# Gelu of a transformer's MLP from Square, Tanh and two VectorE operations instead of one table function

## The chip, the cores and the metric

The kernel runs on one core of a Trainium2 chip. The time is the device time of one execution in microseconds, and of several executions the median counts. The five engines are TensorE (PE; its weight loads are listed as PEld), VectorE (DVE), ScalarE (ACT), GpSimd (POOL) and SyncE (SP), which here only issues the transfers of the DMA queue. Each engine runs its instructions in the order in which the program gives them.

## The reference

Two transformer layers over 2048 rows of 256 numbers, with 16 heads of 16, and with 1601 rows of context in the second layer. All is float32.

```python
# layer 0: adaptive norm from c (ada_w, ada_b), two halves x0, x1 of 1024 rows
x0 = x0 + g_msa[0] * mha(mod(ln(x0), ...));  x1 = x1 + g_msa[1] * mha(mod(ln(x1), ...))
ox = attend(qx, ky, vy) @ crs_proj_w + crs_proj_b    # each half attends to the other
oy = attend(qy, kx, vx) @ crs_proj_w + crs_proj_b
x = x + concat(g_mca[0] * ox, g_mca[1] * oy)
def mlp(z):                                          # 256 -> 1024 -> 256
    return gelu(z @ mlp_fc1_w + mlp_fc1_b, approximate=True) @ mlp_fc2_w + mlp_fc2_b
x = x + concat(g_mlp[0] * mlp(mod(ln(x[:1024]), ...)), g_mlp[1] * mlp(mod(ln(x[1024:]), ...)))
# layer 1
x = layernorm(x + mha(x, x, x, mask))                # masked self-attention
x = layernorm(x + mha(x, ctx, ctx))                  # attention to the context
x = layernorm(x + relu(x @ w1 + b1) @ w2 + b2)
```

`gelu(..., approximate=True)` is 0.5 x (1 + tanh(sqrt(2/pi) (x + 0.044715 x^3))).

## The kernel before

**Stages.** There are four attention stages: 0 (self-attention of the halves), 1 (cross-attention of the halves), 2 (masked) and 3 (context). The rows are cut into four blocks of 512 (`BLK`). A unit of work is one block and one of four groups of four heads, and `stream` runs all units of all stages in one sequence of steps. One step of unit u does four things: the scores of a later unit, for their maxima (`maxima`: two matmuls of L860, then on DVE one reduction, L875, or in the masked stage two pairs of L868); the transposed scores of u, less the maxima (`weights_of`: L938, L945, in the masked stage also L953) with the Exp on ACT (L958); a share of the product with the values (`values_of`: L975); and one piece of background work. Each pair of scores takes one of three PSUM buffers `s_ps`, which L860 and L938 use in turn; the sums of the unit and the background pieces share the two PSUM banks `m0` and `m1`, one each, which change roles from unit to unit. `as_rows` (L899, then the copy `nm` on ACT, L904) also uses the bank of the background work.

**Background.** When the last group of a block is through, `chain_after` hangs a chain of pieces into the background: projection, residual, normalization, the MLP, and keys, values and queries of the next stage. A chain is a generator. A `piece` yields before it takes its bank, then issues its matmuls, yields, and one step later issues what takes the result out of the bank. Steps with other turns on the bank (L899) hold a piece back, and when a unit ends and the bank changes roles, `flush` issues what is unfinished at once. So the chain's place in the order of every engine comes from the number of its yields.

**The MLP.** `mlp` runs for each block twice: with Gelu in `chain_cross` (stage 1, four blocks; the fourth block's chain runs beside the first units of the masked stage), and with Relu in `chain_last`. The first layer has eight pieces: two matmuls (L515) into the bank, then `take` on ACT (L523) with the bias of the column `cols[:, ci + f]` into one of eight tiles `hid`. While `stream` runs, `take` is only an Identity for the Gelu, and the eight Gelus stand inside the second layer, each ahead of the first matmul that reads its tile (L534, L535). The second layer has four quarters of eight tiles (16 matmul records each, L535), and `gated` adds the result to the block (L478 on DVE, L479 and L481 on POOL); then L553 stores the block.

**Start.** Before any stage, SP issues in this order: `c`, the first rows of x, ada weights and biases, more of x, the raw weights of stage 0 (`w_raw`, `w_v`, `bv`), then `cols` (L261, the biases of both first layers) and the small transfers of `qkb` (L269). Meanwhile PE multiplies ada (L284): DVE copies the transposed `c` into `cT` (L278), and each product goes through one bank to DVE (L288). Normalization, products, stores and loads of keys follow in one chain.

**Keys on their way.** The new keys and queries go out as a rounded part and a rest: `hi` on ACT (L392), `lo` on DVE (L393), each into one of three buffers of the tag `half`, from which SP stores them (`k_dr`, `q_dr`, L397). They come back for the next stage as `kT` (L712) and `q` (L771). SP issues all of them in one order with the mask loads (`raw`, L804, two buffers, cast on POOL by L805), the sums (L1013, L1022), their inverses (L1044, L1046) and, in the split first block of the masked stage, the maxima (`mh`, L911). The tag `stage` has two buffers, for the normalized block, the values on their way out, raw weights and context rows.

Of the kernel before, what the change touches and what calls it, by code (L numbers as in the profile page):

```python
# [16 lines left out]
AF = mybir.ActivationFunctionType  # L17
ALU = mybir.AluOpType
# [4 lines left out]
P = 128  # L23
# [6 lines left out]
DFF = 1024  # L30
BLK = 512
# [45 lines left out]
def two_layers(ctx: ExitStack, tc: tile.TileContext, a: dict, out: bass.AP):  # L77
    nc = tc.nc
# [18 lines left out]
    streaming = [False]  # L97
# [13 lines left out]
    def one_ps(dtype=F32, n=None):  # L111
        n = small[0] if n is None else n
        flush((n,))
        return ps.tile([P, BLK], dtype, tag=f"m{n}", bufs=1, name=f"m{n}_ps")
# [3 lines left out]
    def piece(*steps):  # L118

        yield BANK  # L120
        if streaming[0]:
            n = small[0]
            m = one_ps(n=n)
        else:
            n = None
            while len([e for e in unfinished if e[0] is None]) > 2:
                flush_one()
            m = ps.tile([P, 2, BLK], F32, tag="s", bufs=3, name="s_ps")[:, 0, :]
        left = [lambda f=f: f(m) for f in steps[1:]]
        entry = (n, left)  # L130
        unfinished.append(entry)
        steps[0](m)
        while left:

            yield 1 if len(left) > 1 else 0
            if left:
                left.pop(0)()
        if entry in unfinished:
            unfinished.remove(entry)

    def flush_one():
        entry = next(e for e in unfinished if e[0] is None)
        unfinished.remove(entry)
        while entry[1]:
            entry[1].pop(0)()
# [42 lines left out]
    def stage(shape, dtype=F32, name="t"):  # L188
        return sb.tile(shape, dtype, tag="stage", bufs=2, name=name)
# [4 lines left out]
    def hidden(shape, dtype=F32, name="hid"):  # L194
        return sb.tile(shape, dtype, tag="hidden", bufs=HB, name=name)
# [64 lines left out]
    cols = sb.tile([P, 16], F32, tag="cols", name="cols")  # L260
    nc.sync.dma_start(cols, a["cols"][:, 32:])  # L261

    qkb = sb.tile([P, 4, 2, 2], F32, tag="qkb", name="qkb")
    src = a["cols"][:, :32].rearrange("(c i r) (t w g) -> g i c r t w", c=2, i=2, t=4, w=2)
    for g in range(NG):
# [8 lines left out]
    m = one_ps()  # L274
# [6 lines left out]
    for n0, n, w, ada_b in ada:  # L281
        m = one_ps()
# [223 lines left out]
    def mlp(w, ci, func, hT, finish, between=None):  # L506
        w1, w2 = w
        hid: list = [None] * (DFF // P)


        wait = func != AF.Relu and streaming[0]

        def up(m, f):
            for k in range(2):
                nc.tensor.matmul(  # L515
                    m, lhsT=w1[k][:, f * P : (f + 1) * P], rhs=hT[:, k, :],
                    start=k == 0, stop=k == 1,
                )

        def take(m, f):  # L520
            hid[f] = hidden([P, BLK])
            bias = cols[:, ci + f : ci + f + 1]
            nc.scalar.activation(hid[f], m, AF.Identity if wait else func, bias=bias)  # L523

        for f in range(DFF // P):
            yield from piece(lambda m, f=f: up(m, f), lambda m, f=f: take(m, f))
        if between is not None:
            between()

        def down(m, n, q2):  # L530
            qt = 2 * n + q2
            for f in range(DFF // P):
                if wait and qt == 0:
                    nc.scalar.activation(hid[f], hid[f], func)  # L534
                nc.tensor.matmul(  # L535
                    m[:, q2 * D : (q2 + 1) * D], lhsT=hid[f][:, qt * P : (qt + 1) * P],
                    rhs=w2[f // 4][:, f % 4, :], start=f == 0, stop=f == DFF // P - 1,
                )

        for n in range(2):  # L540
            yield from piece(
                *(lambda m, n=n, q2=q2: down(m, n, q2) for q2 in range(2)),
                lambda m, n=n: finish(n, m.rearrange("p (t d) -> p t d", d=D)),
            )
# [41 lines left out]
    def chain_cross(b):  # L586

        last = b == ORDER[1][-1]
        t = residual(x_in(b))
        yield from project(1, b, gated(rows["a1"], t, b))  # L590
        if last:
            load_output(2)
            rows["a2"] = load_rows(7, 3)
        yield 2
        xn = stage([P, TPB, D], name="xn")
        yield from normalize(xn, t, 1e-6)
        hT = yield from transposed(xn, mod=(2, b // 2))
        yield from mlp(
            mlp0, 0, AF.Gelu_apprx_tanh, hT, gated(rows["m0"], t, b),

            (lambda: mask_part(1)) if last else None,
        )
        if last:
            rows["a3"] = load_rows(10, 3)
        kept((2, b), t)
        yield 2
        hT = yield from transposed(t)
        yield from keys_and_values(2, hT, b)
        yield from halves(2, 0, hT, b, BLK)
        if last:  # L610
            background.extend([chain_context(n), 0, False] for n in range(NB))
# [36 lines left out]
    def chain_last(b):  # L648

        t = residual(xs[3, b])  # L650
        yield from project(3, b, biased(rows["a3"], t))
        yield 3
        yield from post_norm(rows["a3"], t)
        hT = yield from transposed(t)
        yield from mlp(mlp1[0], 8, AF.Relu, hT, biased(rows["m1"], t))
        yield 3
        yield from post_norm(rows["m1"], t)
        nc.sync.dma_start(out[b * BLK : (b + 1) * BLK, :].rearrange("(t p) d -> p t d", p=P), t)
# [676 lines left out]
```

## Time and profile before

| | |
|---|---|
| median of 3 runs | 3392.64 us (3391.25 to 3396.46) |
| the profiled execution | 3403.53 us, span 3401.7 us from the first to the last instruction |
| granted TensorE clock, mean over the span | 0.968 |
| busy: PE, DVE, ACT, POOL | 92%, 62%, 50%, 12% of the span |
| transfers of the DMA queue | 187.57 MB, 22.3% of 16 engines' span |
| Gelu (L534), 32 instructions | 17.1 us on ACT, 615 ns each |
| table loads on ACT | 10, at 1283 ns; 4 before a Gelu, 5 before an Exp, 1 before the Silu |

A profile line of a group gives engine, line, operation, what it writes and reads with shapes, how often, the busy time in us and the mean in ns, then the engine's idle time just before these instructions and what ended it. A timeline line gives start, length, engine, line, operation and, in brackets, the idle time before it with what ended it. A busy PE is not PE at its peak, since ends of matmuls are modelled. PE, ACT and DVE work on different steps at once, so the idle time of ACT or DVE costs nothing by itself; idle time of PE does.

### The profile page before, as it was taken

The page shows a single profiled execution, that of the slowest core. Times are in us where ns is not written, and L with a number is a line of the kernel's source. Part 1 is how long each engine was busy: PE and PEld are TensorE (multiplying, and loading weights), DVE is VectorE, ACT ScalarE, POOL GpSimd, SP SyncE. Part 2 cuts the span into 40 slices and gives each one's busy share as a digit, 9 for nine tenths or more (in the row PEclk, how much of TensorE's full clock was granted, in tenths as well). Part 3 has the DMA queues.
Part 4 walks back from the last instruction along what each step waited for, and adds up shares of the span by engine and source line. Part 5 has one row for each costly group of instructions (what it writes and reads, how often), then busy time and mean ns, then how long its engine had stood idle before and what let it go on. Part 6 is the DMA issues. An engine that isn't in the chain of part 4 may idle for free.

```text
span 3401.7 us, 56761 instructions
## 1 busy us (share of the span) xinstructions
PE 3113.2 (92%) x22592; PEld 1362.0 (40%) x22592; DVE 2120.7 (62%) x3858; ACT 1713.7 (50%) x1868; POOL 404.6 (12%) x344
## 2 busy tenths in 40 slices
PE   4799999998999889898999999999999999999995
PEld 2334444444444433333333333343334444444433
DVE  2676766764646455366767777767656747657541
ACT  1265655655545445343555555554546646546461
POOL 0001101101010121104023012201010011110102
PEclk8799999999999999899999999999999999999997
DMA  5652162160204121343111001102241100000000
GB/s 177 140 105 65 36 117 65 48 128 24 65 18 114 32 84 37 94 100 107 51 39 51 15 20 58 32 17 55 49 87 43 26 10 26 25 18 26 10 14 16
DMA packets 162362, 191.20 MB, mean 56 GB/s; under 512 B 82584, under 2 KB 95520, under 8 KB 162096
## 3 DMA queue, kind: packets, MB, share of 16 engines
q1 hardware_dynamic: 162096, 187.57, 22.3%
q8 instruction: 178, 2.92, 0.4%
q14 instruction: 88, 0.72, 0.1%
HBM read 129.91 MB, written 48.46 MB: 52 GB/s over the span
## 4 chain that ended last, share of the span: by engine, by line
PE 51%; DVE 5%; ACT 4%; DMA 2%; SPq 2%; POOL 1%; issue 1%; ACTq 0%; POOLq 0%; DVEq 0%
PE m_ps L975 13%; PE s_ps L938 8%; PE s_ps L860 8%; PE s_ps L953 7%; PE s_ps L945 6%; ACT e L958 3%; PE m_ps L515 2%; DVE s_ps L868 2%; PE m_ps L535 2%; DVE pm L875 1%; PE m_ps L460 1%; DMA raw<-in_mask 1%; PE m_ps L385 1%; DVE t L328 1%; PE m_ps L415 1%
## 5 line engine op out<-in xcount | busy, mean ns | idle before, releaser
L958 ACT ACTIVATE e<-s_ps 128x1024 f32<-128x1024 f32 (+1 forms) x1440 | 1468.1, 1025 | 1375.0 <-PE s_ps L945 794.8
L875 DVE TENSOR_REDUCE pm<-s_ps 128x2 f32<-128x1024 f32 (+3 forms) x1024 | 1120.9, 1106 | 534.7 <-PE s_ps L860 530.2
L975 PE MATMUL m_ps<-e,V 128*32 128x256 f32 (+2 forms) x10432 | 903.6, 418 | 7.3 <-ACT hT L354 4.4
L868 DVE CUSTOM_DVE_ANT_0 s_ps<-s_ps,bias 128x512 f32<-128x512 f32 x1024 | 712.8, 701 | 295.4 <-PE s_ps L860 161.6
L860 PE MATMUL s_ps<-kT,q 64*128 64x512 f32 (+3 forms) x3072 | 676.6, 443 | 111.8 <-ACT e L958 51.1
L938 PE MATMUL s_ps<-q,kT 64*128 64x512 f32 (+1 forms) x2880 | 677.3, 466 | 51.8 <-ACT e L958 28.4
L945 PE MATMUL s_ps<-nm,sel 64*128 64x512 f32 (+1 forms) x2880 | 575.2, 395 | 0.1
L860 PEld LDWEIGHTS s_ps<-kT,q 64*128 64x128 f32 x3072 | 294.1, 186 | 528.1 <-issue 301.1
L938 PEld LDWEIGHTS s_ps<-q,kT 64*128 64x128 f32 (+1 forms) x2880 | 270.5, 184 | 496.6 <-issue 241.0
L975 PEld LDWEIGHTS m_ps<-e,V 128*32 128x32 f32 (+1 forms) x10432 | 206.9, 108 | 433.6 <-issue 415.3
L953 PE MATMUL s_ps<-biasT,ident 128*128 128x512 bf16 x1024 | 311.4, 386 | 0.0
L1053 POOL TENSOR_TENSOR oT<-oT,rd_rows 64x512 f32<-64x512 f32 x64 | 81.7, 1277 | 1904.8 <-DMA rd_rows<-rd_dr 1491.1
L945 PEld LDWEIGHTS s_ps<-nm,sel 64*128 64x128 f32 (+1 forms) x2880 | 275.2, 187 | 12.1 <-ACT nm L904 0.8
L805 POOL TENSOR_SCALAR bias<-raw 128x512 bf16<-128x512 int32 x64 | 123.1, 1924 | 266.4 <-DMA raw<-in_mask 256.4
L868 DVE DVE_READ_ACCUMULATOR2_ANT pm<- 128x1 f32 x1024 | 144.9, 141 | 0.0
L953 PEld LDWEIGHTS <-ident 128*128 128x128 bf16 x1024 | 58.4, 97 | 187.8 <-issue 187.8
L393 DVE SCALAR_TENSOR_TENSOR lo<-m_ps,qkb,hi 128x512 fp32r<-128x512 f32 (+2 forms) x56 | 41.1, 734 | 137.3 <-ACT hi L392 94.3
L535 PE MATMUL m_ps<-w_mlp,hid 128*128 128x256 f32 x448 | 111.4, 405 | 11.9 <-ACT hid L534 11.9
L385 PE MATMUL m_ps<-hT,w_qk 128*128 128x512 f32 (+2 forms) x224 | 109.8, 613 | 9.3 <-DVE lo L393 8.8
L515 PE MATMUL m_ps<-hT,w_mlp 128*128 128x512 f32 x224 | 111.0, 618 | 1.1 <-ACT hT L354 1.1
L535 PEld LDWEIGHTS m_ps<-w_mlp,hid 128*128 128x128 f32 x448 | 86.3, 200 | 36.5 <-ACT hid L534 16.3
L415 PE MATMUL m_ps<-w_v,hT 128*128 128x256 f32 (+1 forms) x212 | 58.0, 420 | 21.8 <-DVE lo L393 21.4
(106 smaller groups left out, 1220.9 us busy)
## 6 DMA issues: line engine op xcount, KB each, us to landing
q<-q_dr SPq DMA_DIRECT2D x544, 64.0 KB
kT<-k_dr SPq DMA_DIRECT2D x192, 128.0 KB
raw<-in_mask SPq DMA_DIRECT2D x64, 256.0 KB
q_dr<-hi SPq DMA_DIRECT2D x32, 256.0 KB
q_dr<-lo SPq DMA_DIRECT2D x32, 256.0 KB
oT<-sums SPq DMA_DIRECT2D x256, 32.0 KB
rd_rows<-rd_dr SPq DMA_DIRECT2D x64, 128.0 KB
v_dr<-v SPq DMA_DIRECT2D x14, 544.0 KB
```

What stands on the lines that cost most here:

```text
L385: nc.tensor.matmul(m[:, :n], lhsT=wqk[:, k, w, c, :], rhs=hT[:, k, :n], start=k == 0, stop=k == 1)
L515: nc.tensor.matmul(m, lhsT=w1[k][:, f * P : (f + 1) * P], rhs=hT[:, k, :], start=k == 0, stop=k == 1,)
L535: nc.tensor.matmul(m[:, q2 * D : (q2 + 1) * D], lhsT=hid[f][:, qt * P : (qt + 1) * P], rhs=w2[f // 4][:, f % 4, :], start=f == 0, stop=f = ...
L805: nc.gpsimd.tensor_scalar(bias_rows[b, slot, qt][:, j * BLK : (j + 1) * BLK], raw, 0.0, MASKED, ALU.is_equal, ALU.mult,)
L860: nc.tensor.matmul(s[:, h, :nn], lhsT=u["q"][64 * h : 64 * h + 64, i, qt * P : (qt + 1) * P], rhs=kT[g][slot][64 * h : 64 * h + 64, i, c : ...
L868: nc.vector.tensor_tensor_reduce(out=s[:, h, :], in0=s[:, h, :], in1=bias_rows[b, slot, qt][:, c : c + nn], scale=1.0, scalar=-3.0e38, op0 ...
L875: nc.vector.tensor_reduce(u["pm"][:, qt, :, i, n], s[:, :, :nn], AX.X, ALU.max)
L938: nc.tensor.matmul(s[:r, h, :], lhsT=kT[g][slot][64 * h : 64 * h + 64, i, kt * P : kt * P + r], rhs=u["q"][64 * h : 64 * h + 64, i, :], st ...
L945: nc.tensor.matmul(s[:r, h, :], lhsT=sel[64 * h : 64 * h + 64, i, :r], rhs=u["nm"][64 * h : 64 * h + 64, :], start=False, stop=not masked,)
L953: nc.tensor.matmul(s[:, h, :], lhsT=ident16, rhs=bias_columns[b, slot, kt], start=False, stop=True,)
L958: nc.scalar.activation(e[:r], s[:r], AF.Exp, scale=SCALE)
L975: nc.tensor.matmul(u["av"][PH * j : PH * (j + 1), cut], lhsT=V[g][slot][:r, kt * GW + j * VW : kt * GW + j * VW + PH], rhs=u["e"][n, j % 2 ...
```

## The change

The Gelu of a tile is now built from functions that need no table of their own. With h = 0.5 (x + bias), which ACT writes as `hid` (Identity with scale 0.5), and s = h squared, which ACT writes as `squares` from the same PSUM bank (Square), DVE makes (s + 0.25/b) h, ACT takes the Tanh of it with the scale 8 a b, and DVE makes (tanh + 1) h, with a = sqrt(2/pi) and b = 0.044715. The steps of one tile are spread over the following ones: `take` of tile f first issues the finish of tile f−3 and the cube of tile f−1 on DVE, then on ACT the Identity of f, the Tanh of f−2 and the Square of f. After the eighth tile one further yield follows, and then what is left of tiles 5 to 7. The squares take buffers of the tag `stage`, two tiles to a buffer. Since the bias enters after the scale, its eight columns are halved once at the start, by one DVE instruction right after the load of `cols`. The Relu's path is left as it was.

```diff
     nc.sync.dma_start(cols, a["cols"][:, 32:])
+
+    nc.vector.tensor_scalar(cols[:, :8], cols[:, :8], 0.5, None, ALU.mult)
...
     def mlp(w, ci, func, hT, finish, between=None):
         w1, w2 = w
         hid: list = [None] * (DFF // P)
-        wait = func != AF.Relu and streaming[0]
+        squares: list = [None] * (DFF // P)
+        gelu = func != AF.Relu
+        b = 0.044715
+        a_ = math.sqrt(2.0 / math.pi)
...
         def take(m, f):
             hid[f] = hidden([P, BLK])
             bias = cols[:, ci + f : ci + f + 1]
-            nc.scalar.activation(hid[f], m, AF.Identity if wait else func, bias=bias)
-
-        for f in range(DFF // P):
+            if not gelu:
+                nc.scalar.activation(hid[f], m, func, bias=bias)
+                return
+            finish_gelu(f - 3)
+            add_cube(f - 1)
+            nc.scalar.activation(hid[f], m, AF.Identity, bias=bias, scale=0.5)
+            take_tanh(f - 2)
+            if f % 2 == 0:
+                t = stage([P, 2, BLK], name="squares")
+                squares[f : f + 2] = t[:, 0, :], t[:, 1, :]
+            nc.scalar.activation(squares[f], m, AF.Square, bias=bias, scale=0.5)
+
+        def add_cube(f):
+            if f >= 0:
+                nc.vector.scalar_tensor_tensor(
+                    squares[f], squares[f], 0.25 / b, hid[f], ALU.add, ALU.mult
+                )
+
+        def take_tanh(f):
+            if f >= 0:
+                nc.scalar.activation(squares[f], squares[f], AF.Tanh, scale=8.0 * a_ * b)
+
+        def finish_gelu(f):
+            if f >= 0:
+                nc.vector.scalar_tensor_tensor(
+                    hid[f], squares[f], 1.0, hid[f], ALU.add, ALU.mult
+                )
+
+        n_f = DFF // P
+        for f in range(n_f):
             yield from piece(lambda m, f=f: up(m, f), lambda m, f=f: take(m, f))
+        if gelu:
+            yield 0
+            finish_gelu(n_f - 3)
+            add_cube(n_f - 1)
+            take_tanh(n_f - 2)
+            take_tanh(n_f - 1)
+            finish_gelu(n_f - 2)
+            finish_gelu(n_f - 1)
         if between is not None:
             between()
...
             for f in range(DFF // P):
-                if wait and qt == 0:
-                    nc.scalar.activation(hid[f], hid[f], func)
                 nc.tensor.matmul(
```

## The prediction

> **What bounds the kernel now.** The shares of busy time and the chain of waits come first: PE is busy 92% of the span, DVE 62%, ACT 50%, and half of the chain that ended last is matmuls. So a change pays where PE stands still, and an instruction added to ACT or DVE costs only where PE comes to wait for it.
>
> ```profile
> PE 3113.2 (92%) x22592; PEld 1362.0 (40%) x22592; DVE 2120.7 (62%) x3858; ACT 1713.7 (50%) x1868; POOL 404.6 (12%) x344
> ...
> PE 51%; DVE 5%; ACT 4%; DMA 2%; SPq 2%; POOL 1%; issue 1%; ACTq 0%; POOLq 0%; DVEq 0%
> ```
>
> The groups by line and form show the Gelu (L534) and its table loads:
>
> ```profile
> L534 ACT ACTIVATE hid<-hid 128x512 f32<-128x512 f32 x32 | 17.1, 615 | 0.0
> L534 ACT ACT_TABLE_LOAD x4 | 5.1, 1283 | 0.1
> L478 DVE TENSOR_TENSOR u<-m_ps,rows 128x512 f32<-128x512 f32 x24 | 16.6, 692 | 59.3 <-PE m_ps L535 29.0 <-PE m_ps L460 17.7 <-ACT e L958 10.6
> ```
>
> The PE timeline of the first Gelu block (columns: start, length, engine, line, idle before) shows the price. The first quarter of the second layer (L535) begins 3.11 us late and then takes 5.58 us; the next, undisturbed, takes 3.72:
>
> ```profile
> 830.94 0.40 PE L945 MATMUL s_ps<-nm,sel 64*128 64x512 f32 x2
> 834.46 5.58 PE L535 MATMUL m_ps<-w_mlp,hid 128*128 128x256 f32 x16 [3.11 <-ACT hid L534]
> 839.97 0.50 PE L860 MATMUL s_ps<-kT,q 64*128 64x512 f32 x2
> ...
> 841.31 0.40 PE L945 MATMUL s_ps<-nm,sel 64*128 64x512 f32 x2
> 841.64 3.72 PE L535 MATMUL m_ps<-w_mlp,hid 128*128 128x256 f32 x16
> 845.29 0.49 PE L860 MATMUL s_ps<-kT,q 64*128 64x512 f32 x2
> ```
>
> Last, the start of the kernel: SP issues the load of `cols` late, and DVE's copy `cT`, which all of the ada products need, is long done by then (from the timelines of DVE, PE, SP and POOL):
>
> ```profile
> 3.39 0.15 DVE L278 COPY cT<-m_ps 128x4 f32<-128x4 f32 x1
> 7.35 3.57 PE L284 MATMUL m_ps<-ada_w,cT 128*2 128x512 f32 x4 [4.46 <-DMA ada_w<-in_ada_w]
> 11.39 0.33 SPq L261 DMA_DIRECT2D cols<-in_cols  x1
> 16.90 1.01 POOL L225 COPY w_qk<-w_raw 128x128 f32<-128x128 f32 x4 [0.28 <-DMA w_raw<-in_w_attn]
> ```
>
> [...] each Gelu group has a load before it and one before the next Exp, at 1283 ns[...]. The built order of the changed kernel has two loads, both before the first MLP. [...] Here 3.11 us were enough (granted clock 0.83 from 831 to 841 us), 2.54 us in the fourth block were not. [...]
>
> **The change part by part.**
>
> *Removed: the Gelu stall.* Undisturbed, L945 to L860 is 845.29 − 841.31 = 3.98 us. Block 1 took 839.97 − 830.94 = 9.03: 5.05 lost. Likewise block 2 (993.45 to 1003.60) lost 6.17, block 3 (1165.89 to 1174.82) 4.95, and block 4, in the masked stage, from L975 at 1352.66 to L860 at 1360.11, 7.45 against 4.22: 3.23. Sum: **−19.4 us**, slow clock and eight table loads included.
>
> *Added on ACT, per tile.* Identity stays (0.69), Tanh of two tiles ago (taken as the Gelu, 0.61) and Square (as Identity, 0.69) stand between it and the Exp. Eight Gelus in a row took 4.26 us, so a follower adds some 0.1 less than its length: Square ends 0.69 + 0.51 + 0.60 = 1.80 after Identity's start. It reads the PSUM bank `m0`, of which there is one, and the next L515 needs it. In stage 1 L523 begins at 826.13 and L515 at 827.69: room of 1.56. With 0.07 of hand-off PE waits 0.3 us, for five tiles of a block (the first two have no Tanh, the last no successor): 1.5 us, three blocks: **+4.5**. In block 4 the room is 1.90 (1347.41 to 1349.31): nothing. The Exp behind it starts where it did (1.73 after Identity), so no other wait comes of it.
>
> *Added on DVE, per tile: two scalar_tensor_tensor.* The trace has the form only from PSUM with a pointer (L393, 751 ns); tensor_tensor is 692. I take 0.69, 0.61 in a row. With one reduction (1.22) that is 2.4 of a 3.58 us step; in the masked stage 2.8 of 3.92. PE hides both. Every operand is a step old when it is used.
>
> *The tail.* After the eighth tile DVE has two finishing operations, a cube and a finish again in a row, the last behind Tanh 7 on ACT, and the next key reduction (L875) queues behind them. From the last Identity's start: reduction done 1.7, finish 5 2.3, cube 7 2.9, Tanh 7 3.8, finish 7 4.6, reduction 5.8. PE, in steps now free of MLP work, wants that score buffer (three in the ring) at 4.2: 1.6 us, three times; in block 4 the reduction is two L868 pairs (1.58) and ends at 6.2, wanted at 4.2: 2.0. **+6.8**.
>
> *The start.* The new halving of `cols` stands before `cT` in DVE's queue, and the `cols` load stands behind both `w_raw`, `w_v` and `bv` in SP's. The second `w_raw` lands at 16.9; 384 KB follow at about 390 GB/s (1 us), then 128 small rows. The trace doesn't show `cols` landing: at the earliest as a lone small load (rd_dr to rd_rows, 2.0 us, so 13.4), at the latest 18.4. I take 17.9: the ada products begin at 18.3, not 7.35. Behind them everything up to the first scores at 86.28 is one chain (mod, normalize, products, k_dr, kT): **+11.0**, bounds +6 and +11.5.
>
> *Moved.* One more yield, and a bank conflict with L899, put the four L535 quarters one or two steps later and the keys, values and queries of the next stage two steps later, against an unchanged stream of SP transfers. Three waits depend on that:
>
> ```profile
> 1218.44 3.49 PE L415 MATMUL m_ps<-w_v,hT 128*128 128x256 f32 x8 [8.69 <-DVE lo L393]
> 1403.80 3.78 PE L415 MATMUL m_ps<-w_v,hT 128*128 128x256 f32 x8 [3.73 <-DVE lo L393]
> 1436.74 0.76 PE L860 MATMUL s_ps<-kT,q 64*128 64x512 f32 x1 [6.58 <-issue]
> ```
>
> The first two are `lo` waiting for a buffer that k_dr still reads, with k_dr behind mask loads on SP. Block 3: k_dr now stands behind five mask loads and rd_rows rather than three, about 7 us more of SP, with the keys some 11 us later: 8.69 falls to about 4.5, **−4.2**. Block 4: SP is through its mask loads some 8 us before the keys: 3.73, the 0.80 that PE waited for POOL at 1387.76, and the slow clock after it (L415 3.78 for 1.99, then 0.7 over the next step) go: **−7.0**. Small ones of the kind in blocks 1 and 2 (0.79, 0.48): **−1.2**. The third is the first key load of the masked stage behind eight L911 transfers: three kT transfers stand behind them now, not one, 0.6 us each: **+1.2**. The x_dr store, the q loads and the mask casts on POOL only change places with one another; each is ready before its reader (t of block 4 about 2 us before its transposes).
>
> Sum: −19.4 + 4.5 + 6.8 + 11.0 − 4.2 − 7.0 − 1.2 + 1.2 = **−8.3 us**. The profiled execution took 3403.53 us (span 3401.7), 0.3% over the median of the runs, 3392.64; the difference is carried over: 3395.2 there, **3384.3** in the median. 0.2%, about what a measurement of this kernel can tell from no change, is 6.8 us.
>
> **The rivals.** *A, the sum above*, −2 to −14: 0.45. *B, the transfers keep their waits*: SP's stalls are as long in the new order, and only the first four terms count: +2.9, 3395.5. For it: the raw ring of two and POOL's 1924 ns casts (L805) are unchanged. Against: the keys come later. 0.20. *C, slower: the Square holds the PSUM bank longer.* If Tanh or Square waits for DVE or runs like a longer form, every 0.3 us past my 0.3 costs 31 tiles × 0.3 = 9 us; it decides from 0.5 us per tile on (+15 on A: 3399.6 and more). At 0.8 it is 3408. For it: 1.80 against a room of 1.56 leaves no slack at all. Against: ACT is busy 2.9 of 3.58 us, DVE 2.4. 0.15. *D, better*: `cols` lands near 13.4 (−5), or block 3's wait goes altogether (−4.5): −13 to −18, 3377. For it: SP issues the load at 11.39. Against: the queue before it is full until 17. 0.20. That the loads stay, so that nothing is saved, is excluded by the built order.
>
> **How the numbers follow.** Some 0.6 of A lies below −6.8 (0.27), the rest within 6.8 (0.18); D is faster (0.20); B is no change but for 0.03; C is slower (0.15). Faster 0.47, same 0.35, slower 0.18. The range takes A, B and most of D, and C only at its beginning: 3372 to 3402.
>
> **What would show it.** Right: no table load after the first Exp; PE idle of about 0.3 before L515 with Square named, 1.6 once per block behind the reduction; L284 begins near 18 us and the first scores near 97; the 3.73 before L415 gone, the 8.69 about halved. Wrong: L284 near 8 us (the start costs nothing), idle before L515 over 0.5 us or Tanh waiting for DVE (C), the 8.69 or a new wait of that kind at full length (B).

## The result, and the profile after

The changed kernel takes 3386.27 us in the median (3374.01 to 3396.21, 20 runs), the kernel before 3397.55 us (3380.96 to 3413.57, 20 runs). The ratio is 0.9965, with an interval of 0.9954 to 0.9976: about 12 us faster, with some 4 us either way. In a later set of runs it was 0.9972 (0.9962 to 0.9982). The prediction was −8.3 us.

The two profiled executions differ by more: 3381.27 us (span 3379.4) against 3403.53. Executions of one kernel spread by 10 to 17 us to either side of the median; the profiled one of before lay on the slow side, that of the changed kernel on the fast side. So a stretch that differs between these two traces is not yet an effect of the change; the start, below, shows how far that can mislead.

Lines of the changed kernel stand 2 higher than before up to the MLP, 5 higher at the first layer and 38 higher behind the MLP's first part: L515 is L520, L535 is L573, L415 and L393 are L417 and L395, L860 is L898, L938 is L976, the Exp L958 is L996. In the experiments they shift by a few more.

From the page's first part, the busy times of the changed kernel; ACT and DVE have more to do, PE less:

```profile
PE 3094.5 (92%) x22592; PEld 1352.8 (40%) x22592; DVE 2156.3 (64%) x3923; ACT 1719.5 (51%) x1892; POOL 404.6 (12%) x344
```

The groups by line and form. The second layer (L573) no longer waits, where it stood idle for 11.9 us before; the first layer (L520) waits for the Square, 3.2 us over fifteen times; the new operations and the only two table loads follow (at 0.72 and 134.28 us; no Tanh, no Square and no Exp behind them brings another):

```profile
L520 PE MATMUL m_ps<-hT,w_mlp 128*128 128x512 f32 x224 | 111.0, 618 | 4.3 <-ACT squares L538 3.2 <-ACT hT L356 1.1
L573 PE MATMUL m_ps<-w_mlp,hid 128*128 128x256 f32 x448 | 104.1, 385 | 0.0
...
L552 DVE SCALAR_TENSOR_TENSOR hid<-squares,hid 128x512 f32<-128x512 f32 x32 | 21.8, 691 | 1.2 <-ACT squares L548 1.1
L538 ACT ACTIVATE squares<-m_ps,cols 128x512 f32<-128x512 f32 x32 | 21.7, 680 | 0.0
...
L548 ACT ACTIVATE squares<-squares 128x512 f32<-128x512 f32 x32 | 19.6, 624 | 0.0
...
L275 ACT ACT_TABLE_LOAD x1 | 1.3, 1283 | 0.7 <-PEq L1360 0.7
L996 ACT ACT_TABLE_LOAD x1 | 1.3, 1283 | 0.0
```

The timeline of PE around the first Gelu block (start, length, line, idle before): 0.84 us once at the tail, a quarter of the usual 3.72 us. Then the value products of block 3 still wait, those of block 4 (1388.96) no longer, and the first keys of the masked stage wait longer than before:

```profile
838.70 0.50 PE L976 MATMUL s_ps<-q,kT 64*128 64x512 f32 x2 [0.84 <-ACT e L996]
...
841.61 3.72 PE L573 MATMUL m_ps<-w_mlp,hid 128*128 128x256 f32 x16
...
1210.42 3.78 PE L417 MATMUL m_ps<-w_v,hT 128*128 128x256 f32 x8 [5.50 <-DVE lo L395]
...
1388.96 1.99 PE L417 MATMUL m_ps<-w_v,hT 128*128 128x256 f32 x8
...
1417.57 0.76 PE L898 MATMUL s_ps<-kT,q 64*128 64x512 f32 x1 [8.77 <-issue]
```

And the start, from DVE's timeline, then PE's: the halving waits 14.40 us for `cols`, `cT` stands behind it, and the ada products (7.35 before) begin at 18.16:

```profile
17.87 0.17 DVE L263 TENSOR_SCALAR cols<-cols 128x8 f32<-128x8 f32 x1 [14.40 <-DMA cols<-in_cols]
17.95 0.15 DVE L280 COPY cT<-m_ps 128x4 f32<-128x4 f32 x1
```

```profile
18.16 3.37 PE L286 MATMUL m_ps<-ada_w,cT 128*2 128x512 f32 x4 [15.27 <-DVE cT L280]
22.64 1.88 PE L286 MATMUL m_ps<-ada_w,cT 128*2 128x512 f32 x4
```

The first scores come at 91.64 us instead of 86.28. Read from this pair of traces, the start costs 5.4 us and not the predicted 11.0. The first two experiments were made for that difference.

### The profile page after: what moved, and what is told of

It reads as the page before. It is cut to its first block, busy times and chain, and to the rows that moved or that the text cites. A ratio compares the mean times of both kernels' runs of the same rounds, so it can differ in the third digit from the quotient of the medians.

```text
span 3379.4 us, 56826 instructions
## 1 busy us (share of the span) xinstructions
PE 3094.5 (92%) x22592; PEld 1352.8 (40%) x22592; DVE 2156.3 (64%) x3923; ACT 1719.5 (51%) x1892; POOL 404.6 (12%) x344
## 4 chain that ended last, share of the span: by engine, by line
PE 58%; DVE 6%; ACT 5%; DMA 3%; issue 2%; POOL 1%; SPq 1%; ACTq 0%; POOLq 0%; DVEq 0%
PE m_ps L1013 15%; PE s_ps L976 9%; PE s_ps L898 9%; PE s_ps L991 7%; PE s_ps L983 6%; ACT e L996 4%; PE m_ps L520 3%; PE m_ps L573 3%; DVE s_ps L906 2%; DVE pm L913 2%; PE m_ps L387 1%; PE m_ps L462 1%; PE m_ps L417 1%; DVE t L330 1%; DMA raw<-in_mask 1%
## 5 line engine op out<-in xcount | busy, mean ns | idle before, releaser
L996 ACT ACTIVATE e<-s_ps 128x1024 f32<-128x1024 f32 (+1 forms) x1440 | 1468.4, 1025 | 1346.0 <-PE s_ps L983 763.6
L898 PE MATMUL s_ps<-kT,q 64*128 64x512 f32 (+3 forms) x3072 | 675.3, 442 | 113.9 <-ACT e L996 51.0
L976 PE MATMUL s_ps<-q,kT 64*128 64x512 f32 (+1 forms) x2880 | 676.7, 466 | 54.4 <-ACT e L996 31.1
L898 PEld LDWEIGHTS s_ps<-kT,q 64*128 64x128 f32 x3072 | 293.4, 186 | 531.4 <-issue 302.3
L976 PEld LDWEIGHTS s_ps<-q,kT 64*128 64x128 f32 (+1 forms) x2880 | 270.2, 184 | 499.7 <-issue 235.0
L395 DVE SCALAR_TENSOR_TENSOR lo<-m_ps,qkb,hi 128x512 fp32r<-128x512 f32 (+2 forms) x56 | 41.1, 734 | 126.6 <-ACT hi L394 94.9
L520 PE MATMUL m_ps<-hT,w_mlp 128*128 128x512 f32 x224 | 111.0, 618 | 4.3 <-ACT squares L538 3.2
L573 PE MATMUL m_ps<-w_mlp,hid 128*128 128x256 f32 x448 | 104.1, 385 | 0.0
L573 PEld LDWEIGHTS m_ps<-w_mlp,hid 128*128 128x128 f32 x448 | 82.9, 190 | 20.7 <-issue 8.5
L394 ACT ACTIVATE hi<-m_ps,qkb 128x512 fp32r<-128x512 f32 (+2 forms) x56 | 37.8, 675 | 73.3 <-PE m_ps L387 63.8
```

The source lines that it names most:

```text
L520: nc.tensor.matmul(m, lhsT=w1[k][:, f * P : (f + 1) * P], rhs=hT[:, k, :], start=k == 0, stop=k == 1,)
L573: nc.tensor.matmul(m[:, q2 * D : (q2 + 1) * D], lhsT=hid[f][:, qt * P : (qt + 1) * P], rhs=w2[f // 4][:, f % 4, :], start=f == 0, stop=f = ...
L898: nc.tensor.matmul(s[:, h, :nn], lhsT=u["q"][64 * h : 64 * h + 64, i, qt * P : (qt + 1) * P], rhs=kT[g][slot][64 * h : 64 * h + 64, i, c : ...
L976: nc.tensor.matmul(s[:r, h, :], lhsT=kT[g][slot][64 * h : 64 * h + 64, i, kt * P : kt * P + r], rhs=u["q"][64 * h : 64 * h + 64, i, :], st ...
L996: nc.scalar.activation(e[:r], s[:r], AF.Exp, scale=SCALE)
```

## The experiments

The theory: the gain is the Gelu's stall (table loads and eight activations in a row), plus what the later place of the second layer does to three waits on transfers, less a fixed price at the start. Its rivals: the table loads alone; the place alone; a start that costs half as much, or nothing. All ratios are to the kernel before, with 95% intervals; microseconds are the ratio on 3397 us.

### The start

`after_again` is the changed kernel unaltered, the measure for the others.

> The changed kernel once more, as the measure for the three beside it. Expected: 0.9965 of the time of before (about -12 us), the first scores of the stream (L898 from kT,q) at 91.6 us, PE waiting 0.2 us before L520 some fifteen times, once per block some 0.8 us before L976.

```diff
 # after_cols_late, to the changed kernel
-    nc.vector.tensor_scalar(cols[:, :8], cols[:, :8], 0.5, None, ALU.mult)   # ahead of cT
...
+    nc.vector.tensor_scalar(cols[:, :8], cols[:, :8], 0.5, None, ALU.mult)   # behind modc
```

> The changed kernel with one DVE instruction moved: the halving of cols stands behind the ada products instead of ahead of cT. Theory: the wait of DVE for the load of cols is the whole cost of the start, so the ada products begin near 7.4 us again, the first scores come at 86.3 us instead of 91.6, and all that follows lies 5.4 us earlier to the end: about -17 us to before, 0.9949. Rival: the later stream of transfers doesn't move with it and a later wait gives the 5.4 us back: first scores at 86.3 us, but the time of the changed kernel, 0.9965.

```diff
 # before_cols, to the kernel before
     nc.sync.dma_start(cols, a["cols"][:, 32:])
+    nc.vector.tensor_scalar(cols[:, :8], cols[:, :8], 1.0, None, ALU.mult)
```

> The kernel before with one instruction more: cols times 1.0 on DVE, ahead of cT, where the changed kernel halves it. Nothing else differs. Theory: ada products begin at 18.2 us instead of 7.4, but the second and third group take 1.9 us instead of 3.4 to 3.6, and the first scores come at 91.6 us instead of 86.3: +5.4 us, 1.0016 of the time of before. Rival (the term of the prediction): first scores at 97, +11 us, 1.0032. Third: the start is given back later, 1.000.

Measured: 0.9930 (0.9912 to 0.9949) with the halving late, against 0.9972 (0.9962 to 0.9982) for the changed kernel beside it: 0.0042, or 14 us, some 7 either way. The kernel before with the one instruction more: 1.0039 (1.0027 to 1.0052), +13 us, 4 either way. Both intervals leave out the 5.4 us of the theory, and both hold the 11.0 of the prediction. The PE timelines tell why the pair of traces said 5.4. First with the halving late, then the kernel before with the instruction:

```profile
7.36 3.42 PE L286 MATMUL m_ps<-ada_w,cT 128*2 128x512 f32 x4 [4.37 <-DMA ada_w<-in_ada_w]
...
11.89 1.88 PE L286 MATMUL m_ps<-ada_w,cT 128*2 128x512 f32 x4
```

```profile
18.98 3.57 PE L285 MATMUL m_ps<-ada_w,cT 128*2 128x512 f32 x4 [16.08 <-DVE cT L279]
...
23.84 3.57 PE L285 MATMUL m_ps<-ada_w,cT 128*2 128x512 f32 x4
...
28.45 1.88 PE L285 MATMUL m_ps<-ada_w,cT 128*2 128x512 f32 x4
```

Of the four large groups of four matmuls, some run at about half speed (3.57 us in these traces where others take 1.88): three in the trace of before, two in that of the kernel before with the instruction, one in those with the halving late and of the changed kernel (both times). Each costs 1.3 to 1.7 us, whether it begins at 7 or at 18 us, and their number is luck of the execution: `after_no_yield` (below), with the changed kernel's start, has two. So traces with equal numbers have to be compared, over all kernels of this document:

| slow groups | first scores, `cT` not held up | first scores, `cT` behind the halving |
|---|---|---|
| one | 81.2 to 82.4 us (3 traces) | 91.6, 92.1 us |
| two | 82.4 to 87.0 us (5 traces) | 94.3, 96.7 us |

The means differ by 10.1 us in the first row and 10.5 in the second: the start costs some 10 us. The pair of traces said 5.4 because the trace of before has two slow groups more, some 3 us; what is left of the difference is no more than the scatter within one field of the table, up to 4.6 us.

### What the Gelu's stall is made of

```diff
 # before_tanh, to the kernel before
-            mlp0, 0, AF.Gelu_apprx_tanh, hT, gated(rows["m0"], t, b),
+            mlp0, 0, AF.Tanh, hT, gated(rows["m0"], t, b),
```

> The kernel before with Tanh in place of the Gelu in its eight activations ahead of L535; the first MLP then computes with tanh instead of gelu. Order, lengths and waits stay, only the function needs no table of its own. Theory: of the 5 to 6 us lost per block the table load ahead of the first activation (1.28 us), the one before the next Exp (1.28) and the slow clock after the wait are the larger part, and eight activations in a row the smaller: the wait before L535 falls from 3.1 to 1.8 us, and 3 us per block go, -12 us in all, 0.9965 of before. Rival: PE is bound by eight activations in a row (4.26 us against 1.9 us of matmuls in the same quarter), and the loads are only a part of it: -5 us, 0.9985.

Measured: 0.9971 (0.9961 to 0.9981), −10 us; the interval holds the theory's 0.9965 and leaves out the rival's 0.9985. In ACT's timeline the eight activations stand without a table load on either side and take what they took (4.26 us before):

```profile
826.97 4.25 ACT L534 ACTIVATE hid<-hid 128x512 f32<-128x512 f32 x8
```

On PE (timeline, then the group) the wait falls from 3.11 to 1.69 us, and the first quarter, which still runs behind the activations, takes 4.33 us (5.49 in block 3, at a granted clock of 0.81; see the end):

```profile
827.64 4.33 PE L535 MATMUL m_ps<-w_mlp,hid 128*128 128x256 f32 x16 [1.69 <-ACT hid L534]
```

```profile
L535 PE MATMUL m_ps<-w_mlp,hid 128*128 128x256 f32 x448 | 107.8, 394 | 6.2 <-ACT hid L534 6.2
```

For this line before had 111.4 us busy and 11.9 idle, the changed kernel 104.1 and 0.0. So of the 19.2 us between them the function's own table is 9.3, and eight activations ahead of one quarter 9.9 (6.2 idle and 3.7 of slowed matmuls), by one trace of each. Neither half is the whole.

### The place of the second layer

The one further `yield` moves the quarters, keys, values and queries, and nothing else in the change does: with it the kernel before has PE's instructions in the order of the changed kernel, and the changed kernel without it has them in the order of before. Two experiments give the other two corners of a square: old Gelu in the new place, new Gelu in the old place.

```diff
 # before_yield, to the kernel before
             yield from piece(lambda m, f=f: up(m, f), lambda m, f=f: take(m, f))
+        if func != AF.Relu:
+            yield 0
```

> The kernel before with the changed kernel's one further yield after the eighth tile and nothing else: the quarters of L535 stand two to three steps later, the keys, values and queries two steps later, just as in the changed kernel; Gelu and its table loads stay. Theory: the waits on transfers change as they did there, whatever the Gelu does: 8.7 to some 5.3 us before L415 in block 3, 3.7 us and 0.8 us in block 4 to nothing, 0.8 us and 0.5 us in blocks 1 and 2 to nothing, the wait for kT from 6.6 to 8.8 us; -8 us, 0.9976 of before. Rival: those waits changed because the blocks came through 5 us faster, not because of the yield: no change, 1.000.

```diff
 # after_no_yield, to the changed kernel
         if gelu:
-            yield 0
             finish_gelu(n_f - 3)
```

> The changed kernel without its one further yield: the finish of the last tiles stands directly ahead of the first quarter of L573, which is back in the place that it has before. Theory: PE waits in the first quarter for the last Tanh and the last finish, some 2.5 us in each of four blocks instead of 0.8 us before L976, and the transfer waits return to 8.7, 3.7, 0.8 and 6.6 us: about +7 and +8 us to the changed kernel, 1.0015 of before. Rival: the yield is only there for the tail and the transfers go with the Gelu: +7 us, 0.999. Second rival: nothing hangs on it, 0.9970.

Measured: the yield alone 0.9984 (0.9975 to 0.9994), −5 us; the changed kernel without it 0.9991 (0.9978 to 1.0004), where its own is 0.9965 and 0.9972. The yield is worth 5 us beside the Gelu (the theory's 0.9976 lies at the edge of the interval, the rival's 1.000 outside) and 7 to 9 us, some 6 either way, beside the new form. Without it the time is that of the first rival, 0.999, and not the theory's 1.0015; what became of the transfer waits, the traces must tell. The form without the place is 0.9991 less the start's 1.0039, −16 us, 6 either way. PE's timeline of the kernel before with the yield has the waits of the changed kernel, 5.31 us in block 3, none before the value products of block 4, and 8.47 us for the first kT (the first group is cut off by the end of the view):

```profile
1218.79 1.65 PE L415 MATMUL m_ps<-w_v,hT 128*128 128x256 f32 x3 [5.31 <-DVE lo L393]
...
1401.08 1.99 PE L415 MATMUL m_ps<-w_v,hT 128*128 128x256 f32 x8
...
1429.38 0.76 PE L862 MATMUL s_ps<-kT,q 64*128 64x512 f32 x1 [8.47 <-DMA kT<-k_dr]
```

The changed kernel without it has those of before (and 6.54 us for the first kT):

```profile
841.92 3.72 PE L572 MATMUL m_ps<-w_mlp,hid 128*128 128x256 f32 x16 [0.21 <-ACT squares L538]
...
1215.49 3.78 PE L417 MATMUL m_ps<-w_v,hT 128*128 128x256 f32 x8 [8.83 <-DVE lo L395]
...
1397.63 2.46 PE L417 MATMUL m_ps<-w_v,hT 128*128 128x256 f32 x8 [2.94 <-DVE lo L395]
```

So the transfer waits go with the place and not with the Gelu, against the first rival. The other half of the theory for this run failed: without the yield the tail costs nothing. The quarter at 841.92 waits 0.21 us, for the Square, and then runs its 3.72 us; the two Tanhs and the four VectorE operations of tiles 5 to 7 run beside it or just ahead of it, the last until 844.00, and only its last matmuls read these tiles. It is the yield that puts the tail beside steps of 1.5 us.

### The waits that the change adds

```diff
 # after_all3: halving late, and
-            nc.scalar.activation(squares[f], m, AF.Square, bias=bias, scale=0.5)
+            nc.scalar.activation(squares[f], hid[f], AF.Square)
...
             take_tanh(n_f - 2)
+            yield 0
             take_tanh(n_f - 1)
```

> The changed kernel with three edits: the halving of cols behind the ada products; Square reads hid (SBUF, written by the Identity just before) and no longer the PSUM bank; one more yield between the Tanhs of tiles 6 and 7 at the tail. Theory: the start gives 5.4 us, the fifteen waits before L520 go (3.2 us), and of the waits on the Exp before L976 (0.8 us, three times, 0.4 in the fourth block) most goes (2 us): about -10.5 us to the changed kernel, 0.9934 of before. Rival: the second layer comes one more step later, and the keys behind it meet the loads of the next stage (kT, 8.8 us) later still: the 10.5 us shrink to 5 or less, 0.995.

Measured: 0.9907 (0.9887 to 0.9927), 8 us better than with the halving late alone (0.9930), with intervals that overlap. It is better than the theory's 0.9934, which had the start at 5.4 us, and the rival's 0.995 lies far outside. The traces show some 5 of the 8 us. The group of the first layer, 4.3 us idle in the changed kernel, has only the share of `hT` left, and the waits on an Exp behind the tails are gone (in blocks 1 to 3 one of 0.17 to 0.20 us on a reduction is left). The order of PE's instructions is the same with the second yield as with one; only the Tanh and the finishing operations lie in two steps instead of one.

```profile
L521 PE MATMUL m_ps<-hT,w_mlp 128*128 128x512 f32 x224 | 111.3, 619 | 0.7 <-ACT hT L357 0.7
```

### What SP's order costs

Two waits are left around the moved part: `lo` in block 3 and the first `kT` of the masked stage. Four kernels take them up.

```diff
 # all3_k_act: the three edits, and
             for i, t in enumerate((hi, lo)):
-                nc.sync.dma_start(d[c, i, :, :n], t[:, :n].bitcast(F32))
+                eng = nc.scalar if w and st == 2 else nc.sync
+                eng.dma_start(d[c, i, :, :n], t[:, :n].bitcast(F32))
```

> The kernel with the three edits (halving late, Square from hid, a second yield at the tail) and a fourth: the keys of the masked stage are stored by transfers that ACT issues, no longer SP. Theory: lo waits in block 3 for a buffer whose store stands behind mask loads in SP's order; issued from ACT it does not, and the 5.1 us before L418 go: 5 us less than with three edits, 0.989 of before, provided ACT's wait for lo (0.8 us) delays no Exp. Rival: the wait comes back at the next transfer in the same order, the first kT of the masked stage (8.8 us there, then 14): no change, 0.9907.

```diff
 # no_yield_k_act: all3_k_act without either yield
         if gelu:
-            yield 0
...
-            yield 0
             take_tanh(n_f - 1)
```

> Halving late, Square from hid, keys of the masked stage stored by ACT, and no yield at all after the eighth tile: the tail of the Gelu stands directly ahead of the first quarter of L573, as in the run without the yield. Theory: the yield brings its gain only through the order of the transfers. With the keys' stores out of SP's order the waits before the value products (8.8 us in block 3, 2.9 us in block 4, 0.8 us) are gone without it too, the first kT waits 6.5 us instead of 8.6, and the tail lies under the first quarter's 3.7 us of matmuls: 1 to 3 us better than with the second yield, 0.989 of before. Rival: the block waits because the keys are simply early for the mask loads; without the yield 8 us return, 0.992.

```diff
 # four_kT_first: all3_k_act, and in as_rows
+            for entry in [e for e in transfers if e[0] == ("keys", 2, 0, 1)]:
+                transfers.remove(entry)
+                entry[1]()
             t = sb.tile([P, 2, 4 * BLK // P], F32, tag="mh", bufs=2, name="mh")
```

> The kernel with the four edits, and the last kT transfers of the first masked group issued ahead of the eight mh transfers instead of behind them. Theory: the 8.6 us that PE waits for the first kT of the masked stage are mostly these eight issues on SP (4.9 us); ahead of them kT comes some 5 us earlier, the wait is 3.7 us, and the time falls by 5 us to 0.9885 of before. Rival: mh comes 1.5 us later and its reader waits instead, or the key store's own landing is what kT waits for: 0.990.

`no_yield_five` is `no_yield_k_act` with the same three lines in `as_rows`.

> The two above together: no yield, keys stored by ACT, kT ahead of mh. Theory: kT waits 6.5 less 4.9, some 1.6 us; 5 us less than without the last edit, 0.9875 of before. Rival: what the two edits give is the same wait, and together they give no more than the better one alone.

| kernel | ratio to before | wait in block 3 | first kT |
|---|---|---|---|
| after_all3 | 0.9907 (0.9887 to 0.9927) | 5.07 us | 8.80 us |
| all3_k_act | 0.9899 (0.9878 to 0.9920) | gone (1.16 us for an Exp) | 8.57 us |
| no_yield_k_act | 0.9921 (0.9901 to 0.9940) | 9.46 us, elsewhere | 6.54 us |
| no_yield_five | 0.9904 (0.9883 to 0.9925) | 9.30 us, elsewhere | none |
| four_kT_first | 0.9873 (0.9854 to 0.9893) | gone (0.50 us for an Exp) | 1.40 us |

With the keys' stores issued by ACT the wait of `lo` in block 3 is gone and doesn't come back at `kT`: counted from each trace's first `nm` copy, the trace lies within 0.4 us of that of after_all3 at the last such copy ahead of block 3's MLP, and 5.9 us earlier from the value products on to the first `kT`. The times can't decide: they differ by 3 us, and the interval holds the rival's 0.9907 too. A small price stands on ACT: an Exp comes behind the issue of the store of `lo`, and PE waits 1.16 us for it:

```profile
1198.05 0.50 PE L901 MATMUL s_ps<-kT,q 64*128 64x512 f32 x2 [1.16 <-ACT e L999]
```

Without the yield the theory failed, and the time is the rival's (0.992): a wait of the same length stands elsewhere. DVE's timeline, then PE's:

```profile
1214.58 0.75 DVE L396 SCALAR_TENSOR_TENSOR lo<-m_ps,qkb,hi 128x512 fp32r<-128x512 f32 x1 [10.92 <-DMA q_dr<-hi]
```

```profile
1216.52 0.79 PE L977 MATMUL s_ps<-q,kT 64*128 64x512 f32 x2 [9.46 <-DVE pm L914]
```

Here it is the `lo` of the queries, whose stores SP still issues behind the mask loads; the key reduction is queued behind it on DVE, and PE behind that. The yield avoids both, the new queue for the keys only one. That the buffer is held by a store late in SP's order is what this pair shows; a fourth `half` buffer, the more direct test, was not tried.

With the kT transfers ahead of `mh` PE's wait falls by 7.2 us, more than the 4.94 us in which SP issues the eight. The SP timelines show why, first of all3_k_act, then of four_kT_first (start, length of the issues):

```profile
1383.71 0.44 SPq L753 DMA_DIRECT2D kT<-k_dr  x1
1386.58 4.94 SPq L952 DMA_DIRECT2D mh<-nm  x8
1391.57 1.51 SPq L753 DMA_DIRECT2D kT<-k_dr  x3
```

```profile
1382.31 1.84 SPq L753 DMA_DIRECT2D kT<-k_dr  x4
1385.18 4.94 SPq L955 DMA_DIRECT2D mh<-nm  x8
```

SP stood idle ahead of the first `mh` too, from 1384.15 to 1386.58, until `nm` was made (ACT's copy runs from 1385.97 to 1386.56); three kT transfers that needed none of it stood behind. Now the last of them is issued at 1384.15 instead of 1393.08, and PE goes on 4.0 us after it (3.6 before).

The two edits on kT and the keys' queue without the yield (no_yield_five) leave PE no wait for kT at all, but keep the 9.3 us before it; its 0.9875 was missed (0.9904). four_kT_first is the fastest of all: 3357.17 us in the median, 0.9873, some 43 us less than before and some 32 less than the changed kernel. Its expected 0.9885 lies within the interval.

## Why the prediction was right, and where not

Forecast −8.3 us, measured −12 and −10, with some 4 us either way. The sum can be checked by stretches: the starts of the `nm` copies are marks in the stream, and the kernels with the changed stream, the halving early or late (three traces), and those with the stream of before, with and without the added instruction on `cols` (two), can be averaged, counted from the first mark. The start is taken from the table above, the last row from the last mark to PE's first use of `kT`.

| stretch | steps of the prediction | predicted | traces |
|---|---|---|---|
| start | ada products behind `cols` | +11.0 | +10.1 to +10.5 |
| block 1 | −5.05 + 1.5 + 1.6 − 0.8 | −2.7 | −2.5 |
| block 2 | −6.17 + 1.5 + 1.6 − 0.4 | −3.5 | −3.7 |
| block 3 | −4.95 + 1.5 + 1.6 − 4.2 | −6.1 | −4.9 |
| block 4 | −3.23 + 2.0 − 7.0 | −8.2 | −10.6 |
| first kT | three transfers behind `mh` | +1.2 | +2.1 |

The traces' sum is −9.3; between the first mark and block 1 another −0.7 lies within the scatter. Single stretches of blocks 1 to 3 vary by up to 2.3 us among the three traces and up to 3.5 between the two (one cause: the projection ahead of block 3's MLP waits 1.9 to 4.7 us for `oT`, in whichever kernel), so a difference of one microsecond there means nothing. Block 4 varies by at most 1.2 us within a group, and its difference to the forecast, 2.4 us, is real; 1.6 of it is the tail, below.

That the sum came so near is in part luck. Three terms were too dear (the tail by 4.0 us, the first layer by 1.3, the start by 0.5 to 0.9), and three too cheap by up to 1 us each (block 3's transfer, the first kT, and the waits behind `u`, below, that the prediction didn't have).

**The Gelu stall**, −19.4, held: L573 runs without a wait, and what it lost before, 11.9 us of idle and 7.3 of slowed matmuls, is gone. The prediction took it as one sum; the runs split it in two halves.

**The first layer**, +4.5, was 3.2: the wait came fifteen times as forecast and in three blocks only, but at 0.20 to 0.23 us instead of 0.3. Square took 680 ns and Tanh 624, each within 2% of what was taken. Rival C had decided from 0.5 us on; it never came near.

**The tail**, +6.8, is the step that failed: 0.84, 0.80, 0.81 and 0.39 us, 2.8 in all, and another releaser. ACT's timeline of the changed kernel, then DVE's:

```profile
835.68 1.02 ACT L996 ACTIVATE e<-s_ps 128x1024 f32<-128x1024 f32 x1
836.58 1.15 ACT L548 ACTIVATE squares<-squares 128x512 f32<-128x512 f32 x2
837.62 1.03 ACT L996 ACTIVATE e<-s_ps 128x1024 f32<-128x1024 f32 x1
```

```profile
838.46 2.35 DVE L913 TENSOR_REDUCE pm<-s_ps 128x2 f32<-128x1024 f32 x2
```

The last Identity starts at 834.00. The first of the two reductions behind the finishing operations (1.22 us each) is done at 839.68, 5.7 us after it, as forecast (5.8). Had PE's scores of 838.70 waited for its buffer, which is the next one if the three are taken in turn, PE would have stood from 837.87 to 839.7, 1.8 us, near the forecast 1.6. But they begin 1.0 us before that reduction ends, and 0.05 us behind the Exp that stands behind the two Tanhs and ends at 838.65; in block 2 it is the same. So at this place the buffers are not taken in turn, though the description of the kernel says so: by these times PE takes that of the Exp, and the reduction's not before 839.95. Why is not shown. The lengths were right and the wrong holder of the ring was priced. That the yield makes this tail, and a place in the quarter's own step would hide it, was missed: the prediction noted that the steps were free of MLP work and didn't ask for a better place.

**The start**, +11.0, held, at 10.1 to 10.5 us, once equal numbers of slow groups were compared. `cols` landed at 17.87, taken as 17.9.

**The moved transfers**: block 3 fell from 8.69 (7.6 to 8.7 in the three traces that have the Gelu's or Tanh's eight activations in the old place) to 5.50 (4.6 to 5.5 in three traces) instead of to 4.5; block 4 and its two followers went altogether; the small ones went, but three new waits of 0.35 us (the sums' products behind `u`) took their place, which the prediction didn't have. The kT wait rose by 2.2 instead of 1.2.

Rival B (the transfers keep their waits) is refuted by the traces with the yield; D by `cols` landing at its late bound and by block 3's wait, which stayed. Rival C's sum let 31 tiles wait, where the prediction itself counts fifteen; no run came to that case.

## What to carry to other kernels

An instruction that waits for a late transfer holds up what stands behind it on its engine (the halving waited 14.40 us, and `cT`, at 3.39 us in the kernel before, came at 17.95), so it belongs where its result is needed: one small halving, moved, was worth 14 us, some 7 either way, as much as the whole change had gained with it in the wrong place (10 to 12). The function with a table of its own cost 9.3 us here, and the bunching made to save loads another 9.9; a form without it lets its steps be spread one per tile (a bunched one was not tried), and the end of that chain should lie beside a long step of the engine that sets the pace (a wait of 0.21 us beside the quarter's 3.72, of 0.84 beside steps of 1.5). When blocks move, look at the stream of transfers that doesn't move with them: a bare yield, meant for the tail or not, brought 7 to 9 us of this change's net 10 to 12, by the medians.

## What was not expected of the hardware

The matmul groups at the start run at about half speed (3.57 us for four instead of 1.88) for one to three groups, differently from execution to execution, while the records show a granted clock of 1.00 over the same stretch (7 to 20 us in the trace of before, three slow groups). In that trace the slow phase lasts from 7.35 to 20.3 us, with gaps of 0.77 to 0.83 us ahead of the transposes between the groups. What slows these groups, and what ends it, is not shown.

A second point bears on the prediction's reading that 3.11 us of idle PE cost clock (granted 0.83 from 831 to 841 us) and 2.54 us did not (1.00 from 1352 to 1362 us). In the traces with the Gelu of before, all nine waits of 3.1 us before a first quarter were followed by slow matmuls (5.50 to 6.71 us for the quarter in the trace of before, where an undisturbed one takes 3.72), but so were two of the three of 2.54 us (5.41 and 5.50 us for the quarter, at a granted clock of 0.83 in `before_cols` and `before_yield`, where the trace of before has 4.34 at 1.00), and one of the three of 1.7 us with Tanh (0.81 from 1158 to 1167 us):

```profile
1160.55 5.49 PE L535 MATMUL m_ps<-w_mlp,hid 128*128 128x256 f32 x16 [1.70 <-ACT hid L534]
```

So the lower clock was seen behind a gap of 1.7 us, and the full one behind a gap of 2.54 us; what decides is not shown.
